# A diffusion stage in which the last two sequences are finished after the attention steps, in two lanes by turns

## The chip, the cores and the metric

The kernel runs on one core of a Trainium2 chip. One program computes four blocks of a network on eight sequences of 512 tokens with 256 features, all in float32. The metric is the device time of one execution in microseconds, taken as the median of several runs. A core has five engines that run side by side, each through a queue of its own that is worked off in order: TensorE (PE) for matrix products and transposes, VectorE (DVE), ScalarE (ACT), GpSimd (POOL) and SyncE (SP), which issues most DMA transfers. An instruction waits at the head of its queue until the semaphores that it names have been raised by other engines or by transfers. A matrix product writes to PSUM, and DVE or ACT copy the result from there into SBUF.

## The reference, cut to what matters

The first two blocks (differential attention; a local attention with a feed-forward part) are not touched. The third is the diffusion, the fourth a mixture of eight experts. `x` has shape (8, 512, 256); `_layernorm` without weights stands around each block.

```python
# third block: y = layernorm(x), then
y = y + token_diffusion(ln1(y)) * gamma1
y = y + channel_diffusion(ln2(y)) * gamma2
x = x + layernorm(y)

def token_diffusion(h):            # 16 heads of 16 features
    qk, v = h @ Wqk, h @ Wv
    logits = (2*qk.qk^T - |q|^2 - |k|^2) / sqrt(16) * tau
    return softmax(logits) @ v @ Wo          # 512 x 512 for each head

def channel_diffusion(h):          # 8 groups of 32 channels
    qk, v = (h @ Wqk_c)^T, (h @ Wv_c)^T
    logits = (2*qk.qk^T - |q|^2 - |k|^2) / sqrt(512) * tau
    return (softmax(logits) @ v)^T @ Wo_c    # 32 x 32 for each group

# fourth block: z = layernorm(x)
gates = softmax(z @ gate_w); two best experts for each token, weights normed
x = x + layernorm(ln(sum of the two experts' results + z))
```

## The kernel before, in words

The attention of the token diffusion is cut into 32 groups `n`, each of four heads of one sequence: four groups to a sequence, sequence by sequence. A group is worked off in four steps `k`, each for 128 of the 512 keys. In a step, `scores` (L1083) makes four matrix products into `tsa`, two PSUM buffers of two heads each out of a pool of three; ACT takes the exponential of both (L1087, tile `te`); and `sums` (L1096) multiplies them with the values into `tpo`, half a group behind. `toc` (L1102) is the copy of a group's sum, and `divide` (L1113 to L1116) turns it (`tpt`) and divides it by the row sums (`trec`, `to`). Every second group `queries` (tiles `tqk`, `tkT`, `tqT`, `tsq`) and, a group later, `squares` (`tq`; L1035 and L1038 on DVE) make the next pair's queries and keys. There are two versions, of which the flag at L954 picks one; with these inputs it is the one called `known`, which needs no row maxima.

Beside the steps run pieces of other sequences, written as generators: each `yield` ends one part, and one call runs one part.

- `prepare(b)` makes the norms, the turned tokens `thT` and the values (`dwv` products) of the next sequence. It is called from the list `ahead`, twice in a group.
- `finish(b, y, o)` is what follows the steps of sequence `b`: the output of the token diffusion is turned (`to`, `toT`) and multiplied by `dwo`; the second norm `th` is made and turned (`chT`); `cqk` and its product with itself (`cpd`) follow; `cpr` spreads the diagonal; then a softmax on DVE and ACT (L915 to L925); `cpw`, `wc`, `cpv` and `wvc` fold the softmax into a weight; that is applied (`pp<-wvc,chT`), and POOL adds the normed result to `x` (L949).
- `gate(b)` norms `x` into `xf`, turns it (`pt<-const,xf`), multiplies it by the gate's weights (`pg`), ranks the experts (`ahead`, `same` on POOL, `rank`, `sel`, `run`, and the product `ppos`), and sends each token's row to its two experts' lists: eight indirect DMAs issued by POOL (L1310). For the last sequence it also makes the table of the experts' tiles.

`finish(b)` is put on the list `between` when the steps of sequence `b + 1` begin, and `gate(b)` behind it once it has ended. `between` is called twice in a step, and a third time in one step of each sequence: 33 calls a sequence. The last sequence has no steps after it: its `finish` and `gate` run after the steps, as `experts` begins, while SP loads the experts' weights (8.4 MB).

The order of instructions on each engine is fixed when the program is built. A planner takes the order of the code as a priority and moves an instruction ahead where it takes its inputs to be there. Most of the products of `scores` are marked to be moved far ahead (`high_priority`), as far as the three buffers allow. All other products share a PSUM pool `ps` of two buffers. What is written after the branch on the flag can't be moved into the branch.

Of the kernel before, what the change touches and what calls it, by code (L numbers as in the profile page):

```python
# [9 lines left out]
F32 = mybir.dt.float32  # L10
# [6 lines left out]
P = 128  # L17
# [103 lines left out]
class Net:  # L121
# [744 lines left out]
    def diffusion(self, nb, rest):  # L866

        nc, g = self.nc, self.dw  # L870
        later = lambda n, b, **k: rest.enter_context(self.tc.tile_pool(name=n, bufs=b, side="right", **k))
        wk, small, ps = later("t_wk", 1), later("t_small", 3), later("t_ps", 2, space=PSUM)
        tiles = lambda x: [x[:, t, :] for t in range(NT)]
        last = (self.hand[0], wk.tile([P, NT, TH, 16], F32, name="tol", tag="tol"))

        def finish(b, y, o):

            yield
            yield
            oT = wk.tile([P, DC, S], F32, name="toT", tag="chT")  # L880
            self.turned(ps, o.rearrange("p t h e -> p t (h e)"), oT)
            yield

            def add(t0, pp):
                nc.vector.tensor_add(y[:, t0:t0 + 2, :], y[:, t0:t0 + 2, :], pp)

            for t0 in range(0, NT, 2):
                self.project(ps, lambda t: [oT[:, c, self.tok(t)] for c in range(DC)], [g["o"][:, c, :] for c in range(DC)], add, [t0])
                yield

            made = self.moments(small, tiles(y))
            yield
            h = wk.tile([P, NT, D], F32, name="th", tag="th")
            self.normed(tiles(y), tiles(h), *made)
            yield
            hT = wk.tile([P, DC, S], F32, name="chT", tag="chT")
            self.turned(ps, h, hT, g["g2"], g["b2"])
            yield
            qk = wk.tile([P, NT, D], F32, name="cqk", tag="cqk", bufs=1)
            for t0 in range(0, NT, 2):  # L900
                self.project(ps, lambda t: [hT[:, c, self.tok(t)] for c in range(DC)], [g["cqk"][:, c, :] for c in range(DC)],
                             lambda t0, pp: self.copy(qk[:, t0:t0 + 2, :], pp), [t0])
                yield
            pd = ps.tile([P, DC, P], F32, name="cpd", tag="ps")
            for i in range(DC):
                self.mm(pd[:, i, :], [(qk[:, t, self.tok(i)], qk[:, t, self.tok(i)]) for t in range(NT)])
            dot = small.tile([P, DC, P], F32, name="dot", tag="dot", bufs=1)
            nc.vector.tensor_copy(dot, pd)
            dg = small.tile([P, DC, P], F32, name="dg", tag="dg", bufs=1)
            nc.vector.tensor_mul(dg, dot, self.ident.unsqueeze(1).to_broadcast([P, DC, P]))  # L910
            yield
            pr = ps.tile([P, DC, P], F32, name="cpr", tag="ps")
            self.mm(pr, [(self.const[:, C_ONE:C_ONE + P], dg)])

            nc.vector.scalar_tensor_tensor(dot, dot, 2.0, pr, ALU.mult, ALU.subtract)  # L915
            for i in range(DC):
                nc.vector.scalar_tensor_tensor(dot[:, i, :], dot[:, i, :], g["ct"][:, i:i + 1],
                                               self.const[:, C_BLK:C_BLK + P], ALU.mult, ALU.add)
            nm = small.tile([P, DC], F32, name="cnm", tag="cnm")
            nc.vector.tensor_reduce(nm, dot, AX.X, ALU.max, negate=True)  # L920
            rs = small.tile([P, DC], F32, name="crs", tag="crs")
            for i in range(DC):
                nc.scalar.activation(dot[:, i, :], dot[:, i, :], AF.Exp, bias=nm[:, i:i + 1], accum_out=rs[:, i:i + 1])
            nc.vector.reciprocal(rs, rs)
            nc.vector.tensor_mul(dot, dot, rs.unsqueeze(2).to_broadcast([P, DC, P]))  # L925
            yield
            yield

            pw = ps.tile([P, DC, D], F32, name="cpw", tag="ps")
            for i in range(DC):  # L930
                self.mm(pw[:, i, :], [(dot[:, i, :], g["co"][:, i, :])])
            wc = wk.tile([P, DC, D], F32, name="wc", tag="wc", bufs=1)
            self.copy(wc, pw)
            yield
            pv = ps.tile([P, DC, D], F32, name="cpv", tag="ps")
            for i in range(DC):
                self.mm(pv[:, i, :], [(g["cv"][:, c, self.tok(i)], wc[:, c, :]) for c in range(DC)])
            wv = wk.tile([P, DC, D], F32, name="wvc", tag="wc", bufs=1)
            self.copy(wv, pv)
            yield  # L940
            yield
            for t0 in range(0, NT, 2):
                if t0:
                    yield
                self.project(ps, lambda t: [hT[:, c, self.tok(t)] for c in range(DC)], [wv[:, c, :] for c in range(DC)], add, [t0])
            made = self.moments(small, tiles(y))
            yield
            self.normed(tiles(y), tiles(y), *made)
            nc.gpsimd.tensor_add(self.xb(b), self.xb(b), y)  # L949
            yield  # L950
            self.between.add(self.gate(b, wk, small, ps))

        self.logs = True
        flag = nc.values_load(self.flag, min_val=0, max_val=1)  # L954
        with self.tc.If(flag > 0) as known:
            self.tokens(nb, True, wk, small, ps, finish, last)
        with known.Else():
            self.tokens(nb, False, wk, small, ps, finish, last)
        self.joint()
        self.between = Between()  # L960
        self.between.add(finish(nb - 1, *last))

    def joint(self):

# [2 lines left out]
    def tokens(self, nb, known, wk, small, ps, finish, last):  # L967
# [5 lines left out]
        with ExitStack() as ctx:  # L973
# [11 lines left out]
                                                           pp.rearrange("p t (h e) -> p t h e", e=16)), first)  # L985

            def prepare(b):
                y = last[0] if b == nb - 1 else wk.tile([P, NT, D], F32, name="ty", tag="ty", bufs=3)
                xs, ys = tiles(self.xb(b)), tiles(y)
                made = self.moments(small, xs)  # L990
                yield
                self.normed(xs, ys, *made)
                yield
                made = self.moments(small, ys)
                yield
                h = step.tile([P, NT, D], F32, name="th", tag="th", bufs=1)
                self.normed(ys, tiles(h), *made)
                yield
                hT = step.tile([P, DC, S], F32, name="thT", tag="thT")
                self.turned(ps, h, hT, g["g1"], g["b1"])  # L1000
                state[b] = y, hT
                yield
                for t0 in range(0, NT, 2):
                    if t0:
                        yield
                    values(b, [t0])
# [98 lines left out]
            def divide(n):  # L1105

                b, h = heads(n)
                if n % 4 == 0:
                    outs["o", b] = last[1] if b == nb - 1 else wk.tile([P, NT, TH, 16], F32, name="to", tag="to", bufs=2)
                oc = outs.pop(n)  # L1110
                pt = ps.tile([P, NT, 4, 32], F32, name="tpt", tag="ps")
                for t in range(NT):
                    nc.tensor.transpose(pt[:, t].rearrange("p h e -> p (h e)"), oc[:, self.tok(t)], self.ident)  # L1113
                rec = small.tile([P, NT, 4], F32, name="trec", tag="trec")
                nc.vector.reciprocal(rec, pt[:, :, :, 16])
                nc.vector.tensor_mul(outs["o", b][:, :, h, :], pt[:, :, :, 0:16],  # L1116
                                     rec.unsqueeze(3).to_broadcast([P, NT, 4, 16]))

            between = self.between = Between()
            ahead = Between()  # L1120
            total = 4 * nb
            self.joint()
# [5 lines left out]
            for s in range(4 * (total + 1) if known else 0):  # L1128
# [18 lines left out]
                if k == 1 and n % 4 == 0 and n < total:  # L1147
                    if n // 4 + 1 < nb:
                        ahead.add(prepare(n // 4 + 1))
                    if n:  # L1150
                        b = n // 4 - 1
                        between.add(finish(b, state[b][0], outs.pop(("o", b))))
                if k % 2:
                    ahead()
                between()
                if k == 2 and n % 4 == 2:
                    between()
            for s in range(0 if known else 8 * (total + 2)):
                n, j = divmod(s, 8)
# [10 lines left out]
                if j == 5 and 0 <= n - 2 < total:  # L1170
                    divide(n - 2)
                    b = (n - 2) // 4
                    if (n - 2) % 4 == 3 and b < nb - 1:
                        between.add(finish(b, state[b][0], outs.pop(("o", b))))
                if j == 6 and n % 2 and n + 1 < total:
                    squares(n // 2 + 1)
                between()
                ahead()
            between.end()


# [172 lines left out]
    def experts(self, nb, rest):  # L1354


        self.between.end()
        self.logs = False
        rest.close()
        with ExitStack() as ctx:  # L1360
# [196 lines left out]
```

## Time and profile before

| what | value |
|---|---|
| time, median of 3 runs (lowest, highest) | 3858.41 us (3852.40, 3862.06) |
| the profiled execution | 3852.22 us, span 3850.4 us |
| TensorE busy over the span, mean granted clock | 3463.0 us (90%), 0.955 |
| DVE, ACT, POOL busy | 2209.5, 1840.8, 1583.2 us |
| a group of sequence 0 with nothing beside it (from `te` to `te`) | 11.09 us |
| a whole sequence in the middle, with `prepare`, `finish` and `gate` beside it | 81.94 us |
| sequence 7, from its first exponential to the start of its `finish` | 87.04 us |
| from there to the experts' first transpose | 73.61 us |

A line of a timeline reads: start and length in microseconds, engine, source line, operation, the tile written and the tiles read, shape, number of instructions merged into the line; in brackets the idle time of the engine just before it and what ended that. Matrix products of float32 leave two records each. A line of a table by stretch gives, for the stretch, each engine's busy time with its number of instructions, then the mean granted TensorE clock, and the share and rate of the DMA engines. L1310 is line 1310 of the kernel before.

### The profile page before, as it was taken

Reading aid. Unit: us, or ns where it says so; the run is one execution under the profiler, and the core shown is the slowest. Engines: PE = TensorE matmul, PEld = TensorE weight load, DVE = VectorE, ACT = ScalarE, POOL = GpSimd, SP = SyncE. Lnnn points to the kernel's source line nnn. Section 1 sums busy time; section 2 is a strip of 40 time slices with the busy share of each in tenths; the row PEclk is TensorE's granted clock in tenths of the full one; section 3 lists DMA queues with packets and bytes.
Section 4 is the critical chain, followed back from the end, with each engine's and each line's share of the span. In section 5 each row is a group of like instructions: output and inputs, shape, how many; then the busy total and the mean of one; then the engine's idle time right before and its main releaser. Section 6 shows DMA issues by size and latency. Waiting matters only on the chain. (4 is left out here: it accounts for less than half of the span.)

```text
span 3850.4 us, 53540 instructions
## 1 busy us (share of the span) xinstructions
PE 3463.0 (90%) x20034; PEld 1885.2 (49%) x20034; DVE 2209.5 (57%) x4364; ACT 1840.8 (48%) x3687; POOL 1583.2 (41%) x1432
## 2 busy tenths in 40 slices
PE   8999999999987999999999999997988888679985
PEld 3344434343424556666666555564444444346554
DVE  6777767776646666665556666663244443344445
ACT  3555555555543444444444444453655555223334
POOL 3676666676654433333333333321012211153333
PEclk9999999999979999999999999998999999789997
DMA  9300000000001000000010000000000000421115
GB/s 343 124 1 7 7 6 1 7 6 1 6 6 34 4 4 4 4 4 25 4 31 12 9 9 9 9 20 23 1 23 23 23 17 17 146 70 53 52 44 166
DMA packets 95137, 130.28 MB, mean 34 GB/s; under 512 B 24702, under 2 KB 73242, under 8 KB 94874
## 3 DMA queue, kind: packets, MB, share of 16 engines
q1 hardware_dynamic: 88346, 108.94, 8.8%
q0 software_dynamic: 6528, 17.87, 1.3%
q8 instruction: 162, 2.65, 0.3%
q14 instruction: 101, 0.83, 0.1%
HBM read 57.40 MB, written 65.18 MB: 32 GB/s over the span
## 5 line engine op out<-in xcount | busy, mean ns | idle before, releaser
L372 ACT ACTIVATE e<-sa 128x1024 f32<-128x1024 f32 (+3 forms) x512 | 359.2, 702 | 337.3 <-PE sa L365 334.7
L393 POOL TENSOR_TENSOR e<-e,e 128x1536 f32<-128x1536 f32 (+2 forms) x192 | 451.6, 2352 | 92.4 <-PE po L388 82.5
L365 PE MATMUL sa<-qT,kT 32*128 32x512 f32 (+3 forms) x2048 | 430.0, 496 | 9.1 <-ACT e L372 8.8
L369 DVE TENSOR_REDUCE spread<-sc 128x2 f32<-128x256 f32 (+3 forms) x512 | 422.4, 825 | 15.6
L355 PE MATMUL sc<-kT,qT 32*128 32x128 f32 (+3 forms) x2048 | 420.3, 491 | 8.9 <-DVE spread L369 5.3
L655 ACT ACTIVATE lp<-lp,lnm 128x256 f32<-128x256 f32 (+1 forms) x512 | 240.1, 470 | 260.6 <-DVE lnm L647 156.2
L659 POOL TENSOR_TENSOR lp<-lp,lrs 128x1024 f32<-128x1024 f32 x64 | 121.1, 1893 | 528.8 <-DVE lrs L656 508.7
L1087 ACT ACTIVATE te<-tsa 128x1024 f32<-128x1024 f32 x256 | 249.0, 1024 | 136.6 <-PE tsa L1083 87.5
L368 DVE TENSOR_TENSOR sc<-sc,const 128x256 f32<-128x256 f32 x512 | 218.6, 427 | 158.6 <-PE sa L365 138.2
L355 PEld LDWEIGHTS sc<-kT,qT 32*128 32x128 f32 x2048 | 159.5, 188 | 282.9 <-issue 126.2
L213 PE MATMUL lpa<-ghT,lw 128*128 128x512 f32 x640 | 284.8, 600 | 12.1 <-ACT ghT L568 12.1
L213 PE MATMUL lqk<-qkv,lhT 128*128 128x512 f32 x512 | 247.8, 622 | 2.3 <-DVE qk L606 1.6
L607 POOL TENSOR_TENSOR qk<-qk,over 128x1024 f32<-128x1024 f32 x64 | 151.4, 2365 | 207.7 <-DVE qk L606 207.7
L375 POOL TENSOR_SCALAR_AFFINE_SELECT e<-e 128x512 f32<-128x512 f32 x256 | 160.4, 640 | 169.3 <-ACT e L372 169.3
L1406 ACT ACTIVATE ehT<-eht,enorm 128x128 f32<-128x128 f32 x288 | 108.2, 457 | 210.0 <-PE eht L1402 202.7
L213 PEld LDWEIGHTS lpa<-ghT,lw 128*128 128x128 f32 x640 | 119.4, 190 | 163.3 <-issue 136.3
L388 PE MATMUL po<-e,v 128*32 128x512 f32 (+3 forms) x2048 | 188.3, 451 | 4.0 <-POOL e L375 3.6
L644 DVE TENSOR_TENSOR lp<-lsc,const 128x768 f32<-128x768 f32 (+1 forms) x128 | 138.7, 1083 | 86.5 <-PE lsc L641 86.0
L641 PE MATMUL lsc<-lkT,lqT 64*128 64x256 f32 (+1 forms) x1024 | 156.6, 386 | 28.1 <-DVE qk L606 28.0
L365 PEld LDWEIGHTS sa<-qT,kT 32*128 32x128 f32 x2048 | 158.9, 189 | 43.4 <-ACT e L372 27.4
L1083 PE MATMUL tsa<-tqT,tkT 32*128 32x512 f32 x1024 | 171.0, 673 | 6.3 <-DVE tqT L1038 3.4
L213 PE MATMUL py<-ew,ehT 128*128 x576 | 145.2, 396 | 24.1 <-ACT ehT L1406 23.7
(293 smaller groups left out, 6799.5 us busy)
## 6 DMA issues: line engine op xcount, KB each, us to landing
xrows<-zero SPq DMA_DIRECT2D x66, 514.0 KB
ex<-xrows SPq DMA_DIRECT2D x72, 128.5 KB
ew<-in_L_ffn_w_dram SPq DMA_DIRECT2D x16, 512.0 KB
egot<-yrows SPq DMA_DIRECT2D x16, 512.0 KB
x<-in_L_attn_X_dram SPq DMA_DIRECT2D x8, 512.0 KB
saved<-x SPq DMA_DIRECT2D x8, 512.0 KB
lx<-saved SPq DMA_DIRECT2D x8, 512.0 KB
xf<-xf SPq DMA_DIRECT2D x8, 512.0 KB
```

The costliest lines, as they stand in the source:

```text
L213: self.nc.tensor.matmul(out, lhsT=l, rhs=r, start=i == 0, stop=i == len(pairs) - 1)
L355: nc.tensor.matmul(sc[:, i, :w], lhsT=qT[g, self.tok(t)], rhs=kT[g, :w], start=True, stop=True)
L365: nc.tensor.matmul(sa[:, i, :S - k * P], lhsT=kT[g, self.tok(k)], rhs=qT[g, k * P:], start=True, stop=True)
L368: nc.vector.tensor_add(sc[:, :, w - P:w], sc[:, :, w - P:w], own)
L369: nc.vector.tensor_reduce(self.spread[n % 2][:, t, g0:g0 + 2, 0 if n % 2 else 16], sc[:, :, :w], AX.X, ALU.max, negate=True)
L372: nc.scalar.activation(x[:, h0:h0 + 2, :], sa[:, :, :S - k * P], AF.Exp, scale=0.25)
L375: nc.gpsimd.affine_select(x[:, :, :P], x[:, :, :P], [[0, 4], [1, P]], ALU.is_ge, 0.0, base=0, channel_multiplier=-1)
L388: nc.tensor.matmul(pos[n][group(g), k * P:], lhsT=seqs[b][1][:, k, 4 * r + g, :], rhs=x[:, g, :], start=k == 0, stop=k == 2)
L393: nc.gpsimd.tensor_add(y, y, es.pop((n, k)))
L655: nc.scalar.activation(x, x, AF.Exp, bias=nm[:, i, k:k + 1], accum_out=rs[:, i, k:k + 1])
L1083: m = nc.tensor.matmul(sa[i // 2][:, i % 2, :], lhsT=kT[q, self.tok(k)], rhs=qT[q, :], start=True, stop=True)
L1087: nc.scalar.activation(e[:, 2 * i:2 * i + 2, :], sa[i], AF.Exp)
```

## The change

`finish` and `gate` of the last two sequences, 6 and 7, are both taken out of the steps and run after them. First twelve parts of sequence 6 run alone, then one part of 6 and one of 7 by turns, until both have ended. Beside the steps of sequence 7 (groups 28 to 31) no `finish` or `gate` runs, but what may be left of sequence 5. Sequence 6 keeps its `y` in the tile `thl` (free since the first sequence) and its output in a new tile `tom`. So that two lanes can be under way at once, sequence 7 takes its tiles `toT`, `chT`, `cqk` from the three buffers of `ty` and `th` from that of `to`, which has one buffer in place of two. Tiles of `gate`, among them `xf` with one buffer, are the same for both lanes. `gate` is now the end of `finish` itself and not a piece put at the end of the list. And `between` gets its third call in one step of every group, 36 calls a sequence.

```diff
-        last = (self.hand[0], wk.tile([P, NT, TH, 16], F32, name="tol", tag="tol"))
+        last = {nb - 2: (self.hand[1].rearrange("p c (u d) -> p (c u) d", d=D), wk.tile([P, NT, TH, 16], F32, name="tom", tag="tom")),
+                nb - 1: (self.hand[0], wk.tile([P, NT, TH, 16], F32, name="tol", tag="tol"))}
         def finish(b, y, o):
+            tag = lambda k, other: (dict(tag=other, bufs=bufs[other]) if b == nb - 1 else dict(tag=k, bufs=1))
+            bufs = dict(ty=3, to=1)
             yield
             yield
-            oT = wk.tile([P, DC, S], F32, name="toT", tag="chT")
+            oT = wk.tile([P, DC, S], F32, name="toT", **tag("chT", "ty"))
...
-            self.between.add(self.gate(b, wk, small, ps))
+            yield from self.gate(b, wk, small, ps)
...
         self.joint()
-        self.between = Between()
-        self.between.add(finish(nb - 1, *last))
+        lanes = [finish(b, *last[b]) for b in (nb - 2, nb - 1)]
+        for _ in range(12):
+            next(lanes[0])
+        while lanes:
+            for p in list(lanes):
+                if next(p, self) is self:
+                    lanes.remove(p)
...
                 if k == 1 and n % 4 == 0 and n < total:
                     if n // 4 + 1 < nb:
                         ahead.add(prepare(n // 4 + 1))
-                    if n:
-                        b = n // 4 - 1
+                    b = n // 4 - 1
+                    if 0 <= b < nb - 2:
                         between.add(finish(b, state[b][0], outs.pop(("o", b))))
                 if k % 2:
                     ahead()
                 between()
-                if k == 2 and n % 4 == 2:
+                if k == 2:
                     between()
...
     def experts(self, nb, rest):
-        self.between.end()
```

`prepare` and `divide` take `y` and `o` of sequences 6 and 7 from the new table `last`. The other version of the steps, which does not run with these inputs, is changed in the same way.

More of the change, by code (lines that the diff above doesn't have):

```diff
@@ L892, in finish @@
             yield
-            h = wk.tile([P, NT, D], F32, name="th", tag="th")
+            h = wk.tile([P, NT, D], F32, name="th", **tag("th", "to"))
             self.normed(tiles(y), tiles(h), *made)
             yield
-            hT = wk.tile([P, DC, S], F32, name="chT", tag="chT")
+            hT = wk.tile([P, DC, S], F32, name="chT", **tag("chT", "ty"))
             self.turned(ps, h, hT, g["g2"], g["b2"])
             yield
-            qk = wk.tile([P, NT, D], F32, name="cqk", tag="cqk", bufs=1)
+            qk = wk.tile([P, NT, D], F32, name="cqk", **tag("cqk", "ty"))
             for t0 in range(0, NT, 2):
@@ L987, in prepare @@
             def prepare(b):
-                y = last[0] if b == nb - 1 else wk.tile([P, NT, D], F32, name="ty", tag="ty", bufs=3)
+                y = last[b][0] if b in last else wk.tile([P, NT, D], F32, name="ty", tag="ty", bufs=3)
                 xs, ys = tiles(self.xb(b)), tiles(y)
@@ L1108, in divide @@
                 if n % 4 == 0:
-                    outs["o", b] = last[1] if b == nb - 1 else wk.tile([P, NT, TH, 16], F32, name="to", tag="to", bufs=2)
+                    outs["o", b] = last[b][1] if b in last else wk.tile([P, NT, TH, 16], F32, name="to", tag="to", bufs=1)
                 oc = outs.pop(n)
@@ L1117, in divide @@
                                      rec.unsqueeze(3).to_broadcast([P, NT, 4, 16]))
-            between = self.between = Between()
+            between = Between()
             ahead = Between()
@@ L1172, in tokens @@
                     b = (n - 2) // 4
-                    if (n - 2) % 4 == 3 and b < nb - 1:
+                    if (n - 2) % 4 == 3 and b < nb - 2:
                         between.add(finish(b, state[b][0], outs.pop(("o", b))))
@@ L1178, in tokens @@
                 ahead()
+                if j == 7:
+                    between()
             between.end()
```

## The prediction

> **What bounds the kernel now.** I read the page's busy times first, then a table of stretches, then TensorE's timeline in one middle sequence and behind the steps, and last POOL's timeline there. In the table, the columns behind the stretch are its length, the busy times of PE, PEld, DVE, ACT and POOL, and the granted clock.
>
> ```profile
> 2702.93:2714.02 11.09, 11.09 (x74) 3.38 (x72) 3.31 (x6) 8.04 (x9) 0.00 (x0) 1.00 0.00 0
> 2978.67:3060.61 81.94, 72.41 (x434) 36.66 (x430) 35.50 (x113) 46.87 (x68) 15.00 (x18) 0.96 0.06 20
> 3225.99:3313.03 87.04, 70.88 (x420) 33.81 (x412) 27.87 (x86) 42.12 (x58) 20.50 (x23) 0.89 0.10 33
> 3313.03:3386.64 73.61, 34.03 (x125) 26.41 (x125) 27.12 (x90) 7.35 (x18) 14.63 (x17) 0.66 0.59 183
> ```
>
> A bare group of steps keeps TensorE busy all of its 11.09 us. A middle sequence takes 81.94 us, TensorE busy for 72.41, so 9.5 us are gaps. Sequence 7 takes 87.04 up to the start of its finish (third row), and the stretch after it 73.61, in which TensorE is busy for less than half: a chain of single operations. So beside the steps TensorE's products count, and the gaps at which its queue stands; behind the steps the chain's length counts.
>
> The middle sequence on TensorE:
>
> ```profile
> 3017.94 0.70 PE L213 MATMUL cpr<-dg,const 128*128 128x256 f32 x2
> 3018.57 3.64 PE L1096 MATMUL tpo<-te,tv 128*32 128x512 f32 x32
> 3022.32 1.10 PE L213 MATMUL cpw<-dwco,dot 128*128 128x256 f32 x4
> ...
> 3030.67 3.72 PE L213 MATMUL pp<-wvc,chT 128*128 128x256 f32 x16 [0.45 <-ACT thT L209]
> ...
> 3045.11 1.12 PE L213 MATMUL tq<-tsq,const 128*128 128x512 f32 x2 [2.29 <-ACT tv L984]
> ...
> 3047.92 0.66 PE L205 MATMUL pt<-const,xf 128*128 128x128 f32 x4 [0.62 <-ACT toc L1102]
> ```
>
> The softmax between `cpr` and `cpw` takes 3.68 us (3018.64 to 3022.32) and is covered by a group's `tpo`. Between the end of `pp<-wvc` (3034.4) and `pt<-xf` lie 13.5 us of other products, so the norms in between are covered too. In sequence 7 that cover was thinner:
>
> ```profile
> 3274.03 3.72 PE L213 MATMUL pp<-wvc,chT 128*128 128x256 f32 x16
> ...
> 3288.22 1.44 PE L205 MATMUL pt<-const,xf 128*128 128x128 f32 x4 [4.47 <-DVE xf L194]
> 3289.60 2.09 PE L1083 MATMUL tsa<-tqT,tkT 32*128 32x512 f32 x8
> ```
>
> Here TensorE stood for 4.47 us: the two norms and the addition on POOL took 10.5 us from 3277.75 on.
>
> Behind the steps:
>
> ```profile
> 3338.92 2.05 PE L213 MATMUL cpw<-dwco,dot 128*128 128x256 f32 x4 [3.28 <-DVE dot L925]
> ...
> 3358.66 2.10 PE L205 MATMUL pt<-const,xf 128*128 128x128 f32 x8 [9.02 <-DVE xf L194]
> ```
>
> The same two waits stand bare, 3.28 and 9.02 us. And POOL:
>
> ```profile
> 3311.77 0.96 POOL L1310 DMA_INDIRECT xrows<-xf,slots  x1 [0.30 <-issue]
> 3318.84 0.52 POOL L1249 TENSOR_SCALAR xf<-const 128x4 f32<-128x4 f32 x2 [6.11 <-DMA xrows<-xf,slots]
> 3353.44 2.34 POOL L949 TENSOR_TENSOR x<-x,tyl 128x1024 f32<-128x1024 f32 x1 [34.08 <-DVE tyl L194]
> ```
>
> The next sequence's `xf<-const` writes the buffer that the scatters read, so it waits until they have landed, and `x<-x,tyl` is queued behind it.
>
> **The change part by part.** *1. Sequence 7 without filler: a gain.* Four groups at the 11.09 of the first row are 44.4. Then come the last half group of `tpo` (3.64), `toc` 0.58, `tpt` 0.66, the division 0.7 and their hand-overs 0.6, and the 2.5 from the end of the division to the first transpose (3310.55 to 3313.03), so 53; I add 1 for the one `queries`. 87 - 54 = 33 us saved.
>
> *2. Behind the steps: a loss.* Today the chain there is 73.6. In the changed order TensorE has sequence 6's products up to `cpv`, and only then `pt<-tol` of sequence 7. Up to the end of `cpv` the chain is today's, 3345.07 - 3313.03 = 32.0. Then sequence 7's own 73.6 run, with sequence 6's rest among them:
> - `pp<-wvc` (3.7) between its `dwo` products, and on DVE the other lane's additions, statistics and norm (about 4) ahead of its norm: 6.5 together up to `pt<-th`;
> - `pt<-xf` (2.1) and `pg` (3.6) ahead of its `cpr`, with `dg` on DVE queued behind `enm`, which waits for `pg`; of the 5.7 about 1 falls into waits that are there today, and 0.8 of DVE work is added: 5.5;
> - `enm`, `ep`, `same`, `rank`, `run` between its softmax operations on DVE, 1.7; `ppos` 0.3 beyond the present wait of 0.85.
>
> That is 14. Then POOL: sequence 6's eight scatters (3302.80 to 3312.73, so 9.9), the landing (6.1 in the row above, beside the weights' load; 2.2 at 2989.98 without one) and `xf<-const` 0.5 stand ahead of sequence 7's `x<-x,tyl`. Measured from the end of sequence 7's `cpv`, the slots are there after 2.7, so `x<-x,tyl` starts after 2.7 + 9.9 + 2.2 + 0.5 = 15.3; by its own chain it could after 8.4 + 0.3 = 8.7. Queued behind the late addition are `same`, `ahead` and the scatters, which the experts' first rows wait for. I take the landing without load, since the weights are in by then (3352): +6.6; with load +10.5. Together 32 + 14 + 6.6 = 52.6; I take **52**, bounds 40 (half of the 14 hidden, no wait on POOL) and 60. SP's loads start where they do today and end before the longer chain does, so they cost nothing.
>
> *3. The steps of sequences 1 to 6: a loss.* Three calls more in a sequence, and `gate` without its one empty call, put the parts closer together. In the changed order:
> - `cpw` follows `cpr` directly, and `tpo` comes after it. The softmax is bare: 3.28 (tail row) to 3.68 (middle); I take 3.4. Ahead of `cpr` there are two products of `tsa` instead of four (0.57 less) to cover `dg`: 0.6.
> - From `pp<-wvc` to `pt<-xf` there are `tpt` 0.66, three times `tsa` 1.14 and the transposes of `th` 1.09: 5.2 for a chain of 9.0 (tail) to 10.5 (sequence 7). 5.3 bare; today 2.0 (0.45, 0.62 and a second 0.96): 3.3. On ACT an exponential (1.02) now stands between the norm's logarithm and its own exponential: 4.3.
> - On DVE the four operations of `squares` come behind `rank`, `sel` and `run`. From the end of `pg`: 4.6 to the end of `run` (3364.73 to 3369.36), 0.2 for its copy, 2.7 for the four: 7.5 until a `ps` buffer is free for the second `dwv`; the products between are 4.1. 3.4 bare, less the 1.0 before `ppos` that goes: 2.4.
> - `tqk` waits for `xT` behind the copy of `xf` (1.04) and a norm's pair on ACT, and `pg` behind `toc` and four exponentials: 1.0 and 1.2, of which I take 2.
> - Gone are the wait for `th` (1.89, at 3006.21) and that of `tq` (2.29): -4.2.
> - The clock. The row is 0.96 in the middle sequence, that is some 3.3 us lost, and behind the gap of 4.47 eight `tsa` products took 2.09 where 1.14 is usual. The Trainium skill ("TensorE: Matmul & The Clock Gate", Part 1) says that the array falls to half its clock after an idle window of 3.4 us and stays there until a busy one has passed. By the rule each of three gaps of 3.4 to 5.3 could cost one window, 1.7 each, 5 a sequence; by the row the one gap cost about 2, part of it within other waits. The windows run freely and the gaps are about as long as one, so not each is hit: I take 2.
>
> 0.6 + 3.4 + 4.3 + 2.4 + 2 - 4.2 + 2 = 10.5 a sequence, six sequences: **63**. Bounds: 3 a sequence (shorter chain, no clock, waits on ACT hidden), 18; and 15 (clock by the rule, later ACT), 90.
>
> *4. Without a price:* `to` with one buffer: the next sequence's first division comes a group after `pt<-to` has read it. The tile `tom` and the tags move no data.
>
> *The sum.* 63 - 33 + 52 = 82. On the profiled execution's 3852.2 that is 3934; it lies 6.2 below the median, so **3940 us** for the median.
>
> **The rivals.**
> - *Only the ends change* (12 in 100). The gaps in the steps are made up by other work, because ACT and DVE are half idle: -33 + 52 = 19, so 3877. For it: the planner placed these products where it took them to be ready. Against it: TensorE works in order, and both waits are seen bare today.
> - *Faster* (5 in 100). Lane 7 truly overlaps lane 6 behind the steps. It would have to start at part 12 (25.9 behind the first transpose), lose nothing by sharing, and the addition on POOL would have to come before the scatters have landed: the stretch grows by 26, less than the 33 saved; with a middle sequence shorter by 1 that gives 3845. It decides where the growth is under 33 and the steps cost nothing. Against it: `pt<-tol` is behind `cpv` at 32.0 already.
> - *More of everything* (13 in 100): 15 a sequence, and the landing at 6.1: 90 - 33 + 60 = 117, so 3975.
> - My case has 70 in 100. That the parts don't move is excluded by the program's order.
>
> **How the numbers follow.** The bounds of parts 2 and 3 give 3858 + 18 - 33 + 40 = 3883 and 3858 + 90 - 33 + 60 = 3975. The range of 3880 to 3978 leaves out most of the first rival, the second and the tail of the third. A change under 0.3% (11.6 us) can't be told from none by these runs. Slower: my case, the third rival and most of the first, 0.93; same 0.02; faster 0.05.
>
> **What would show it.** Right: a middle sequence of about 92 us, with TensorE idle some 3.4 ahead of `cpw`, 5 ahead of `pt<-xf` and 3 ahead of the second `dwv`; sequence 7 at about 54 up to the first transpose; then some 126 to the experts' first transpose, with `x<-x,tyl` on POOL released by the landing of scatters. Wrong: middle sequences of 82 or less, or a stretch behind the steps under 107.

## The result, and the profile after

The changed kernel takes 3951.32 us (median of 4 runs, 3945.92 to 3958.39) against 3858.32 of the kernel before: 93.0 us longer, ratio 1.024 with an interval of 1.0225 to 1.0254. 3940 had been forecast, with a range of 3880 to 3978.

By stretches, each from a first exponential to the next, or to the first transpose behind the steps:

| stretch | before | after | difference | forecast |
|---|---|---|---|---|
| sequences 1 to 6 | 484.2 | 567.2 | +83.0 | +63 |
| sequence 7 up to the first transpose | 87.0 | 53.4 | -33.6 | -33 |
| from there to the experts' first transpose | 73.6 | 119.6 | +46.0 | +52 |
| sum | 644.8 | 740.2 | +95.4 | +82 |

The profiled execution is longer by 106.2; 12.3 of that lie ahead of the steps, where nothing was changed, and the experts' stage gives back 1.4. Both kernels run once more, on a chip where the kernel before takes 3861 us, gave 487.9, 86.1 and 73.6 against 567.1, 53.4 and 119.9.

The table by stretch of the changed kernel (length, then busy PE, PEld, DVE, ACT and POOL, the granted clock, share and rate of the DMA): a middle sequence, sequence 7, and the stretch behind the steps.

```profile
3034.86:3130.37 95.51, 82.08 (x434) 40.09 (x430) 35.04 (x113) 46.86 (x69) 14.96 (x18) 0.89 0.05 17
3321.18:3374.57 53.39, 47.98 (x299) 15.06 (x291) 6.04 (x14) 35.46 (x40) 8.74 (x12) 0.93 0.08 27
3374.57:3494.21 119.64, 64.75 (x247) 50.29 (x247) 50.23 (x163) 14.31 (x36) 26.22 (x28) 0.67 0.39 125
```

The middle sequence holds the same 434 matrix records as before, but they are busy for 82.08 us instead of 72.41, and the clock is 0.89 instead of 0.96. Idle time has grown by less: 13.4 from 9.5.

TensorE's timeline in that sequence, at the places that the prediction named:

```profile
3046.01 5.37 PE L213 MATMUL pp<-dwo,toT 128*128 128x256 f32 x16 [1.27 <-ACT toT L160]
...
3071.51 1.13 PE L1092 MATMUL tsa<-tqT,tkT 32*128 32x512 f32 x4
3072.65 0.67 PE L213 MATMUL cpr<-dg,const 128*128 128x256 f32 x2
3076.60 1.95 PE L213 MATMUL cpw<-dwco,dot 128*128 128x256 f32 x4 [3.28 <-DVE dot L929]
3078.48 2.71 PE L1105 MATMUL tpo<-te,tv 128*32 128x512 f32 x16
...
3090.24 1.14 PE L1092 MATMUL tsa<-tqT,tkT 32*128 32x512 f32 x8
...
3092.48 2.81 PE L1092 MATMUL tsa<-tqT,tkT 32*128 32x512 f32 x12
3096.42 1.37 PE L1092 MATMUL tsa<-tqT,tkT 32*128 32x512 f32 x4 [1.13 <-ACT te L1096]
3100.09 2.30 PE L205 MATMUL pt<-const,xf 128*128 128x128 f32 x8 [2.30 <-DVE xf L194]
3102.31 2.08 PE L1092 MATMUL tsa<-tqT,tkT 32*128 32x512 f32 x4
3104.32 3.51 PE L213 MATMUL tqk<-thT,dwqk 128*128 128x512 f32 x4
...
3124.13 3.47 PE L213 MATMUL pp<-dwv,thT 128*128 128x256 f32 x8 [3.90 <-DVE tqT L1047]
```

`cpw` stands bare for 3.28 us and the second `dwv` for 3.90. Ahead of `pt<-xf` it is 2.30 (and 1.13 ahead of the `tsa` before it). After each of the waits the products are slow: four records of `cpw` take 1.95 where 1.10 was usual, `tqk` 3.51 where it takes 1.88 elsewhere, `dwv` 3.47 in place of 1.99. The table by stretch, cut at these places, shows why; first the changed kernel, then the kernel before:

```profile
3046.00:3049.40 3.40, 3.39 (x8) 2.77 (x9) 0.13 (x1) 1.80 (x2) 0.24 (x2) 0.50 0.00 0
3076.70:3080.10 3.40, 3.40 (x12) 1.34 (x16) 0.00 (x0) 0.59 (x1) 0.00 (x0) 0.50 0.02 5
3097.25:3107.45 10.20, 7.90 (x18) 3.15 (x16) 6.34 (x25) 3.34 (x7) 0.00 (x0) 0.50 0.15 53
3124.50:3127.90 3.40, 3.40 (x12) 2.74 (x10) 0.20 (x1) 0.27 (x1) 0.00 (x0) 0.50 0.00 0
```

```profile
2989.60:2993.00 3.40, 2.89 (x7) 2.36 (x8) 0.62 (x1) 2.30 (x3) 0.45 (x2) 0.50 0.00 0
3006.70:3010.10 3.40, 3.40 (x16) 1.47 (x15) 1.39 (x5) 1.91 (x3) 0.00 (x0) 0.50 0.00 0
```

These are all the stretches of the two sequences in which the clock is at half: 20.5 us after, 6.8 before. Each follows a wait by at most a few microseconds. By the first column of busy times, TensorE works in them for 18.1 us after and 6.3 before.

The rows of `tsa` show a second loss, which has nothing to do with the clock. Eight records of it, the four products of a step, take 1.14 us; but four records, two products, take 1.13 as well. In the trace the four products of a whole group start within 0.02 us of each other (at 3014.26 in the kernel before), so they run side by side; a group that is split takes twice as long. The middle sequence has twelve such pairs after the change and six before. Outside the stretches at half clock, its 128 records of `tsa` take 22.4 us after and 19.1 before.

Behind the steps, TensorE and then POOL:

```profile
3440.53 2.04 PE L213 MATMUL cpw<-dwco,dot 128*128 128x256 f32 x4 [4.21 <-DVE run L1298]
...
3447.88 5.82 PE L213 MATMUL pp<-wvc,chT 128*128 128x256 f32 x16 [0.16 <-DVE wvc L162]
3466.67 2.10 PE L205 MATMUL pt<-const,xf 128*128 128x128 f32 x8 [12.96 <-DVE xf L194]
```

```profile
3458.07 0.96 POOL L1321 DMA_INDIRECT xrows<-xf,slots  x1 [0.30 <-issue]
3460.86 0.51 POOL L1260 TENSOR_SCALAR xf<-const 128x4 f32<-128x4 f32 x2 [1.82 <-DMA xrows<-xf,slots]
3461.45 2.34 POOL L953 TENSOR_TENSOR x<-x,tyl 128x1024 f32<-128x1024 f32 x1
```

As forecast, `x<-x,tyl` stands behind `xf<-const`, and that behind the landing of the other lane's scatters.

### The profile page after: what moved, and what is told of

Same layout as the page of the kernel before. It is cut to its first block, busy times and chain, and to the rows that moved or that the text cites. A ratio compares the mean times of both kernels' runs of the same rounds, so it can differ in the third digit from the quotient of the medians.

```text
span 3956.6 us, 53562 instructions
## 1 busy us (share of the span) xinstructions
PE 3543.1 (90%) x20034; PEld 1915.6 (48%) x20034; DVE 2207.0 (56%) x4364; ACT 1843.1 (47%) x3687; POOL 1584.0 (40%) x1432
## 5 line engine op out<-in xcount | busy, mean ns | idle before, releaser
L1092 PE MATMUL tsa<-tqT,tkT 32*128 32x512 f32 x1024 | 198.4, 665 | 14.7 <-ACT te L1096 8.1
```

Of the source, the lines that this page charges most:

```text
L1092: m = nc.tensor.matmul(sa[i // 2][:, i % 2, :], lhsT=kT[q, self.tok(k)], rhs=qT[q, :], start=True, stop=True)
```

## The experiments

The theory: the loss in sequences 1 to 6 comes from the pacing (more calls in a sequence, `gate` without its empty call), by bare waits and by the clock behind them; the ends are worth -33.6 + 46.0, and the 46.0 come from the two chains lying in series. Ratios are always against runs of the kernel before on the same chip. That kernel takes 3858 to 3861 us on some chips and 3832 on others.

### The old pacing with the new ends

```diff
-            yield from self.gate(b, wk, small, ps)
+            if b < nb - 2:
+                self.between.add(self.gate(b, wk, small, ps))
+            else:
+                yield from self.gate(b, wk, small, ps)
...
-            between = Between()
+            between = self.between = Between()
...
-                if k == 2:
+                if k == 2 and n % 4 == 2:
```

> The changed kernel with the pacing of before in the steps of sequences 1 to 6 (the third call in the third group only, gate put on the list); the two last sequences still run in turn behind the steps. My theory, that the 83.0 us of the steps come from the pacing and the ends are worth -33.6 + 46.0: middle sequences of 82.0 us, sequence 7 at 53.4, 119.6 behind the steps, so 3858.3 + 12.4 = 3871, and half-clock windows of some 7 us in a middle sequence. Rival, that the single buffer of to or the absence of sequence 6's parts costs the steps: middle sequences stay above 88, so over 3905.

Measured: 3842.96 against 3831.73, so +11.2 us, ratio 1.0033 (1.0025 to 1.0042). Two middle sequences, sequence 7, and the stretch behind the steps:

```profile
2818.28:2893.86 75.58, 68.23 (x434) 34.79 (x430) 35.48 (x113) 46.47 (x68) 15.20 (x18) 1.00 0.06 22
2893.86:2972.91 79.05, 72.71 (x434) 37.90 (x430) 35.50 (x113) 46.46 (x68) 15.05 (x18) 0.94 0.06 21
3204.39:3252.94 48.55, 44.68 (x298) 14.11 (x290) 6.04 (x14) 35.04 (x40) 8.93 (x12) 1.00 0.10 31
3252.94:3373.56 120.62, 66.04 (x246) 51.09 (x246) 50.24 (x162) 14.31 (x36) 26.20 (x28) 0.66 0.39 123
```

The lengths that were expected (82.0 a sequence, 3871 in all) missed, because this chip runs the kernel before 27 us faster too. The difference counts: the ends alone cost 11.2, where 12.4 was expected from the two stretches, so the steps' loss is the pacing's. The rival of buffers and missing parts, which had over 3905, falls. The first row is a yardstick as well: with the clock at 1.00, the 434 records take 68.23 us.

### The new pacing alone

```diff
-            self.between.add(self.gate(b, wk, small, ps))
+            yield from self.gate(b, wk, small, ps)
...
-                if k == 2 and n % 4 == 2:
+                if k == 2:
```

> The kernel before with the pacing of the change alone (a third call in every group, gate run within finish instead of put on the list); sequence 6's parts stay beside sequence 7. My theory: the middle sequences take 95.5 us as in the changed kernel, six of them +83.0, and sequence 7 grows as well, from 87.0 to 90 to 95 up to the first transpose of its outputs, the stretch behind it stays at 73.6: 3858 + 83 + 3 to 8 = 3944 to 3950. Rival, that the steps' growth needs the other parts of the change: within 12 us of 3858.

Measured: 3929.15 against 3831.73, +97.4, ratio 1.0246 (1.022 to 1.0271). A middle sequence, sequence 7, behind the steps:

```profile
3025.22:3117.36 92.14, 80.48 (x434) 38.80 (x430) 35.03 (x113) 46.68 (x69) 14.97 (x17) 0.89 0.05 18
3301.53:3390.56 89.03, 77.46 (x420) 35.64 (x412) 27.61 (x86) 42.31 (x58) 18.36 (x21) 0.84 0.09 29
3390.56:3464.46 73.90, 34.58 (x124) 26.57 (x124) 27.10 (x89) 7.35 (x18) 16.43 (x19) 0.66 0.59 187
```

The two pacing lines alone make the whole loss and leave the stretch behind the steps as it was. With the 11.2 of the ends that is 108.6 on this chip, where the whole change cost 93.0 on another; the changed kernel did not run on this one, so the difference stays open. On this chip a middle sequence took 92.1, not 95.5; the second run of the changed kernel, on a chip where the kernel before takes 3861, showed 95.5 again:

> The kernel before once more, on the chip that the runs beside it use, for its stretches there: against the first profile (sequences 1 to 6 at 484.2 us together, sequence 7 at 87.0, 73.6 behind the steps) my theory, by which the run with the old pacing differs from it by -33.6 + 46 only, wants about 462, 84 and 74 here, with half-clock windows of 0 to 10 us in a sequence; a rival, that the old pacing gains in the steps from what else the change does, wants 484 again.

> The changed kernel once more, on the chip that the runs beside it use: by the pacing alone (92.2 us a middle sequence) sequences 1 to 6 should take 553 us here, sequence 7 some 49 to 53 and 120 behind the steps, and the time stand 90 to 100 us over that of the kernel before. If the sequences take 567 again, the difference of 14 belongs to the change's other parts.

They gave 3858.57 and 3949.35 in one run each (the stretches stand in the first section). So 567 came again, and both expectations, which carried one chip's lengths to another, missed. The second of them would put the 14 us between 553 and 567 on the change's other parts. That isn't shown, for the chip could make them as well: with the old pacing and the new ends, sequences 1 to 6 take 461.8 on the first chip and, in the run with close lanes below, 484.5 on this one. Which of the two it is stays open.

### Without the third call

```diff
-                if k == 2:
+                if k == 2 and n % 4 == 2:
```

> The changed kernel without the added third calls; gate still runs within finish. It tells which edit of the pacing makes the loss. My theory names the softmax between cpr and cpw, and the norms ahead of the first transpose of xf, as bare because the third call puts them close together: with fewer calls cpw should again have products of tpo ahead of it, the middle sequence falls to 82 to 88 us, and the time to 3871 to 3910. Rival, that gate within finish is what costs (its one empty call gone, so that every part comes earlier): it stays at 93 to 96 us and 3940 to 3955.

Measured, as the theory had it: 3873.38 against 3831.73, +41.7, ratio 1.0099 (1.0068 to 1.013), and 82.0 us for a middle sequence. Sequences 1 to 6 take 491.3, where the run with the old pacing on the same chip has 461.8. Its middle sequence on TensorE:

```profile
3114.66 0.70 PE L213 MATMUL cpr<-dg,const 128*128 128x256 f32 x2
3115.29 3.64 PE L1105 MATMUL tpo<-te,tv 128*32 128x512 f32 x32
3119.07 1.10 PE L213 MATMUL cpw<-dwco,dot 128*128 128x256 f32 x4
...
3142.20 1.03 PE L205 MATMUL pt<-const,xf 128*128 128x128 f32 x3 [3.48 <-DVE xf L194]
```

`tpo` covers the softmax again, so the third call is what laid `cpw` bare. It also split the groups of `tsa`: a middle sequence has four pairs here, as in the run with the old pacing, and ten in the run with the new pacing alone. `gate` inside `finish` lays `pt<-xf` bare (3.48) without it, and that edit costs 41.7 - 11.2 = 30.5 us, 5 a sequence.

### Filling two of the waits

```diff
+            for _ in range(7 if b < nb - 2 else 0):
+                self.mm(pw[:, 0, :], [(self.ident, g["co"][:, 0, :])])
...
-        self.turned(ps, xf, xT)
+        self.turned(ps, xf, xT, fill=4 if b < NB - 2 else 0)
```

The argument `fill` of `turned` stands for so many products of 128x512 into its first PSUM tile, ahead of the transposes.

> The changed kernel with products added that fill two of the gaps and do nothing else: seven more products of 128x256 into the tile of cpw ahead of its own, and four more of 128x512 into the first tile of the transposes of xf, for sequences 0 to 5; what they write is overwritten. Theory that the clock makes most of the 13.6 us a sequence (the half-clock time went from 6.8 to 20.5 us): the windows behind the gaps at cpw and xf vanish, TensorE's old products take some 75 us again instead of 82, and a middle sequence takes 89 to 93 us although it holds more work, so 3910 to 3940. Theory that the gaps themselves make it and the clock only goes along: 95 to 97 us, so 3951 to 3962.

Measured: 3900.04 against 3831.73, +68.3, ratio 1.0176 (1.015 to 1.0202), and sequences 1 to 6 take 517.8, where the run with the new pacing alone has 553.3 on the same chip. The row of a middle sequence, and TensorE's timeline in it:

```profile
3090.20:3176.23 86.03, 79.00 (x454) 40.53 (x452) 35.03 (x113) 46.57 (x68) 14.83 (x18) 0.98 0.05 19
```

```profile
3123.98 3.18 PE L215 MATMUL cpw<-dwco,const 128*128 128x256 f32 x14
...
3128.09 1.13 PE L215 MATMUL cpw<-dwco,dot 128*128 128x256 f32 x4
...
3143.66 3.70 PE L215 MATMUL pt<-const 128*128 128x512 f32 x8 [0.55 <-ACT thT L211]
3148.93 1.74 PE L207 MATMUL pt<-const,xf 128*128 128x128 f32 x8 [1.57 <-DVE xf L194]
3150.59 1.14 PE L1096 MATMUL tsa<-tqT,tkT 32*128 32x512 f32 x8
3151.93 1.98 PE L215 MATMUL tqk<-thT,dwqk 128*128 128x512 f32 x4 [0.20 <-ACT xT L160]
...
3168.96 3.68 PE L215 MATMUL pp<-dwv,thT 128*128 128x256 f32 x8 [3.89 <-DVE tqT L1051]
```

The added products take 6.9 us (3.18 and 3.70) and the sequence is shorter by 6: 86.0 where the same pacing has 92.1 on this chip. `cpw` is back at 1.13 and `tqk` at 1.98; `dwv`, ahead of which nothing was filled, stays at 3.68. Busy without the added products is 72.1 instead of 80.5. TensorE works at half clock for 3.4 us instead of 17.6, which explains 7.1 of these 8.4. The planner also moved a half group of `tpo` and four products of `tsa` (eight pairs instead of ten); the other 1.3 us are for that and what else moved. Both expectations took 95.5 for the sequence without the added products. Set against the 92.1 of this chip, the theory of the clock has 85.6 to 89.6 and that of the waits alone 91.6 to 93.6. So an idle TensorE costs twice: the wait, and the half clock behind it.

### Closer lanes

> The old pacing, and behind the steps the two lanes closer together and without shared buffers: four parts ahead instead of twelve, the last lane's xf in the two tiles of tv that the steps have left, and a PSUM pool of its own. My theory, that behind the steps the twelve parts ahead put the two chains in series and that the last lane's xf waits for the other's scatters: each lane now fills the other's waits, so that the stretch behind the steps falls from 120.6 us to 73.6 + some 14 of the other lane's products + 10 of its scatters on POOL = 98, and with -34 for sequence 7 the time comes to 10 us under the kernel before (ratio 0.997). Rival, that the two chains take the same engines' time whatever their distance (DVE and ACT hold the chain, not their order): 115 to 121 us, ratio 1.002 to 1.003.

```diff
+        if b == NB - 1:
+            both = [v.rearrange("p t h e -> p t (h e)")[:, :, 0:D + 1] for v in self.tv]
...
+        lanes = [finish(nb - 2, *last[nb - 2]), finish(nb - 1, *last[nb - 1], later("t_ps7", 2, space=PSUM))]
-        for _ in range(12):
+        for _ in range(4):
```

(The first two lines are in `gate`.) Measured: 3894.19 against 3860.7, ratio 1.0086 (1.007 to 1.0101), and 133.3 us behind the steps: a miss, and the rival's 115 to 121 missed too. The chain itself did as expected, the last slots came 74.0 us after the first transpose instead of 105.9. But then:

```profile
3418.57 1.09 PE L1404 MATMUL ext<-const,ex 128*128 128x128 f32 x4 [60.61 <-DMA ex<-xrows]
```

```profile
3373.76 3.98 SPq L1222 DMA_DIRECT2D ew<-in_L_ffn_w_dram  x8
3377.79 14.16 SPq L1224 DMA_DIRECT2D ew<-in_L_ffn_w_dram  x8
```

The load of the experts' weights was issued at 3373.76, 88.5 us into the stretch; in the run with the old pacing it was issued 2.7 ahead of the first transpose. The weights reuse the memory of `tv`, and that was now read by the last scatter, which POOL issued until 3371.87. The loads, and the gather `ex<-xrows` behind them in SP's queue, waited for it. With other memory for `xf`:

```diff
-            both = [v.rearrange("p t h e -> p t (h e)")[:, :, 0:D + 1] for v in self.tv]
+            both = [wk.tile([P, NT, D + 1], F32, name="xf", tag="ty", bufs=3) for _ in range(2)]
```

> As the run with close lanes, but the last lane's xf lies in two buffers of ty, which the experts' weights don't reuse, instead of in tv, which they do. There the slots of the last sequence were ready 74.0 us after the first transpose (105.9 with twelve parts ahead), and then the weights' load stood bare, because it waited until the last scatters had read tv. My theory: the load starts with the stretch again and is in before it ends, and the stretch is 74 + 12.5 for the scatters still queued + 4 to the experts' first transpose = 90.6 (120.6 in the run with old pacing and twelve ahead): 11 - 30 = 19 us under the kernel before, ratio 0.995. Rival, that scatters and landings take longer beside the load of 8 MB that now lies beside them: 100 to 105, ratio 0.998 to 1.000.

Measured: 3813.42 against 3832.27, 18.9 us faster than the kernel before, ratio 0.9952 (0.9936 to 0.9969). The stretch behind the steps, and the weights' load:

```profile
3260.33:3351.43 91.10, 52.34 (x246) 43.87 (x246) 48.24 (x162) 14.69 (x36) 25.73 (x28) 0.74 0.52 163
```

```profile
3257.62 5.69 SPq L1222 DMA_DIRECT2D ew<-in_L_ffn_w_dram  x8
```

91.1 us, where 90.6 was worked out: the change's idea, with the old pacing and short lanes, is worth having. To tell distance from buffers:

> As the run with own rows (close lanes, the last lane's xf in ty, a PSUM pool of its own: 91.1 us behind the steps), with twelve parts ahead again instead of four. It tells the two parts of that gain of 29.5 us apart: distance, or buffers. My theory: distance. With twelve ahead the one lane's gate still stands where the other's norms and its softmax are waiting, so that only the wait of POOL for the landing (3.9) and the last lane's first products (about 7, which now run in the waits of the other lane) go: 107 to 112 us behind the steps, ratio 0.999 to 1.001. Rival, the buffers: 91 to 98 us, ratio 0.995 to 0.997.

Measured: ratio 1.0002 (0.9993 to 1.001), 112.3 us behind the steps, close to the 107 to 112 of the theory of distance. Of the 29.5 us that the stretch lost, 21.2 came from the distance of four instead of twelve parts, and 8.3 from the buffers and the order that they allow.

### Filling waits of the kernel before

> The kernel before with products added in four waits of the last sequence behind the steps (4, 4 and 12 of 128x512 ahead of the transposes of tol, th and xf, 8 of 128x256 ahead of cpw; overwritten). Behind the steps the clock is 0.66, and products take up to twice their time. Theory that idle TensorE is what lowers the clock: the stretch of 73.6 us loses some 9 of its 34 us of products, so 64 to 68, and the time 6 to 9 us (ratio 0.998). Rival, that the added products stand in the way, or the clock stays low: 74 to 80 us, ratio 1.000 to 1.002.

The additions are made as in the run that fills two waits. Measured, as the theory had it: 3854.57 against 3860.7, ratio 0.9981 (0.997 to 0.9991). Sequence 7 and the stretch behind the steps:

```profile
3232.68:3322.09 89.41, 73.73 (x428) 35.16 (x421) 28.05 (x87) 42.25 (x58) 20.51 (x23) 0.90 0.14 46
3322.09:3387.59 65.50, 41.45 (x174) 28.40 (x173) 26.96 (x88) 7.35 (x18) 14.61 (x17) 0.85 0.60 188
```

```profile
3317.47 5.21 PE L215 MATMUL pt<-const 128*128 128x512 f32 x8 [3.43 <-issue]
```

73.6 became 65.5 at a clock of 0.85 instead of 0.66, with nothing taken out of the chain. 3.3 of the 8 went back in sequence 7: the products ahead of `tol` could not begin until the 3.43 had passed, so they came on top (5.21). The same in the steps:

> The kernel before with products added in waits of the steps too: four of 128x256 ahead of the first dwo product and three of 128x512 ahead of the transposes of th in every sequence, five ahead of the transposes of sequence 6's xf, and those of the run with the filled tail. A middle sequence of before has two half-clock windows (6.8 us), each right behind one of these two waits (0.88 + 1.23 and 1.89 us); a sequence with the same products and none of them took 75.7 us. Theory of the clock: both windows go, sequences 1 to 6 take 455 to 465 us instead of 484, behind the steps 65: 25 to 40 us faster, ratio 0.990 to 0.994. Rival, that the sequences' length is set by their waits and the windows are only where the time shows: 82 us stays, and only the tail's 6 to 8 us are gained, ratio 0.998.

> The close lanes with the last lane's rows in ty, and the added products in the steps ahead of dwo and th, and four ahead of the first transpose behind the steps. If the two gains add up: 19 for the ends and 20 to 28 for the steps, ratio 0.988 to 0.990. If one of them fails, the time of the other alone.

Both missed, and the rivals too: 1.0022 (1.0012 to 1.0031) and 0.9992 (0.9984 to 1.0001). In the second run the added products took back 16.6 of the 18.9 us that the run with own rows had gained. On that chip sequences 1 to 6 of the run with own rows, which has the old order, had taken 459.6 with half-clock time in three of the six only; with the added products they took 472.5 and 471.9. There was little to win, and the added products cost some 2 us a sequence. A middle sequence of the first run, with 14 records more than the 434:

```profile
3066.90:3144.70 77.80, 73.78 (x448) 37.73 (x444) 35.55 (x113) 46.69 (x68) 15.02 (x18) 0.98 0.06 21
```

What they do on a chip where a middle sequence takes 82 stays open.

## Why the prediction was right, point by point

**Sequence 7: right.** -33.6 for -33, the one row of a bare group carried it.

**Behind the steps: right, with sizes off that partly cancel.** The end of sequence 6's `cpv` lies 32.0 us after the first transpose, as forecast. The rest grew by 14.0 and not by 14 + 6.6. Up to `pt<-th` 6.1 came (6.5 forecast). `pt<-xf` and `pg` ahead of `cpr` cost 1.1 and not 5.5: they ran where the lane's own waits for `cqk` and `dg` had been. The softmax cost 0.9 for 1.7, `cpv` to `wvc` 0.35. Then 6.1 up to `pt<-xf`: POOL's wait, 3.9 from the end of the norm (3457.56) to `x<-x,tyl` (3461.45) for the 6.6 forecast, and 2.1 because `pp<-wvc` took 5.82 and not 3.72, in a stretch whose clock is 0.67. Behind `pt<-xf` 0.5 came back.

**The steps: right in kind, a quarter too small, and with some luck.** A middle sequence grew by 13.6 us for the 10.5 forecast, and the parts of the sum were further off than the sum:

- *The waits, 3.9 for 8.5.* `cpw` (3.28 for 3.4) and `dwv` (3.90 for 3.4) were right. Ahead of `pt<-xf` the two waits make 3.4 and not 5.3, because the `tsa` products between `pp<-wvc` and it took 5.3 us instead of the 3.4 counted as cover. The waits of `tqk` and `pg` (2) and of `cpr` (0.6) didn't come. For `cpr` the forecast let two products of `tsa` take half the time of four; they took 1.13, as long as four.
- *The clock, 5.9 for 2.* This term was mis-sized most. TensorE works at half clock for 11.8 us more than before, and half of that is lost.
- *What was left out, 3.8.* The same records took 9.7 us longer (82.08 for 72.41); with the clock's 5.9 taken off, 3.8 remain. 3.3 of them are `tsa` outside the half-clock stretches: there are six pairs more than before, and each takes about 0.56 longer than its half of a whole group. The forecast moved products about but kept their lengths. The run with the old pacing bears this out: from its 68.23, at full clock and with four pairs, 9.1 for the half clock and eight more pairs lead to 81.8, and 82.08 was measured.

The waits were 4.6 too large, the clock 3.9 and the split groups 3.8 too small, so a good part of the errors cancelled. Over the six sequences the growth is 16.2, 14.3, three times 13.6, and 11.8 us: 83.0.

The rule of the Trainium skill that was weighed there ("TensorE: Matmul & The Clock Gate", Part 1: an idle window of 3.4 us drops the clock, a busy one restores it) gave 5, which is near the 5.9, while the row of a single gap gave 2. But the windows don't come as that rule has them: two waits of 0.73 and 1.27 close together were followed by a half-clock stretch as well, and at `pt<-xf` three windows came in a row (10.2 us). TensorE was busy for 2.27 of the 3.40 us ahead of these three (3093.77 to 3097.17), so that window was far from idle; the wait of 2.30 lies in the first of them.

**The rivals.** "Only the ends change" is what the run with the old pacing measures: +11.2 for the forecast's +19. "More of everything" had 15 a sequence and a landing of 6.1 us: the steps, at 13.8 on average, came nearer to it than to my 10.5, but the landing took 1.82. The faster rival failed where it was said to: 46.0 of growth is over the 33.6 saved. With four parts ahead the growth is 17.5 (91.1 for 73.6), and there the kernel is indeed faster.

## What to carry to other kernels

A wait of an otherwise busy TensorE should be priced at its length plus the slower products behind it, about 1.7 us for each half-clock window of 3.4 us, and several windows when waits follow one another. Products that run side by side should stay together: a `tsa` group in two pairs took twice as long as in one piece. Parts that are called faster than the work between them can cover lay their own waits bare: 36 calls a sequence in place of 33, and one empty call less, cost 97 us. And when a chain is made shorter or a buffer put elsewhere, look at what reuses its memory next: with `xf` in `tv` the weights' load came into the open, 133.3 us in place of 91.1.

## What was not expected of the hardware

- **Lengths that snap to a grid.** In the trace's record of the clock every stretch at half clock within the run is 3.413 us long or a multiple of it, on one grid throughout the run. The middle sequences take 81.94 (24.0 windows) before, 95.51 (28.0) after, 92.14 (27.0) with the new pacing alone, and sequences 3 to 5 repeat to within 0.1. A reading that fits, but is only argued: a sequence that is hit takes a whole number of windows, so the next begins at the same point of the grid and is hit in the same places. Sequences that were not hit take 75.4 to 75.7 (22.1 to 22.2 windows) and wander. It would explain why the same order takes 82 on one chip and mostly 76 to 79 on another, and the 27 us between the two times of the kernel before.
- **A norm on DVE beside an addition on POOL.** The four operations of a norm take 1.38 us, but took 3.40 where POOL's `x<-x,thl` (2.44, from 3419.64) began just behind the first:

```profile
3418.17 1.38 DVE L194 TENSOR_SCALAR thl<-thl,mv,rs 128x256 f32<-128x256 f32 x4 [0.65 <-ACT rs L170]
3419.47 3.40 DVE L194 TENSOR_SCALAR th<-tyl,mv,rs 128x256 f32<-128x256 f32 x4
```

One of the four, begun 0.15 us after POOL's addition, took 2.43 instead of 0.40 and ended 0.14 after it. That agrees with what the Trainium skill states ("SBUF — State Buffer", "SBUF: two separate sides"): a POOL operation, and a DVE operation of the kinds that use the port pair shared with POOL, lock that pair for the whole instruction, and the other waits.
